# Masking x1 instead of the adjacency in the second aggregation of a two-layer graph kernel

## The chip, the cores and the metric

The kernel runs on one core of a Trainium2 chip. The core has a matrix engine (PE, with its weight loads shown apart as PEld), a vector engine (DVE), a scalar engine (ACT), a third elementwise engine (POOL) and a queue that issues transfers (SP). The time is the device time of one execution in microseconds. Before the change it is 1818.78 us, the median of three runs (1818.59 to 1822.25).

## The reference

There are 64 graphs of 256 nodes with 512 features in float32. Layer 0 aggregates x over the adjacency, divides by the degree, concatenates with x and multiplies by a weight, then adds x and normalizes. Layer 1 projects x1 to q, k and v, aggregates the masked k over the adjacency, takes the dot of q with the aggregate as a score, a softmax over the nodes of a graph, and adds the weighted v before a second normalization.

```python
def _L0_gnn_ref(x, adj, W):
    deg = jnp.sum(adj, axis=-1, keepdims=True)
    agg = jnp.einsum('bij,bjf->bif', adj, x) / jnp.maximum(deg, EPS)
    cat = jnp.concatenate([x, agg], axis=2)
    out = jnp.einsum('bnf,of->bno', cat, W)
    return jax.nn.relu(out)

def _L1_gnn_ref(X, adj, mask, Wqk, Wv):
    qk = X @ Wqk
    q, k = jnp.split(qk, 2, axis=-1)
    v = X @ Wv
    k_m = k * mask[:, :, None]
    agg = jnp.einsum('bij,bjd->bid', adj, k_m)
    w = inv_scale * mask * jnp.einsum('bid,bid->bi', q, agg)
    L = jax.nn.softmax(w, axis=1)[:, :, None] * v
    return L

x = _layernorm(x + _L0_gnn_ref(x, adj, L0_gnn_W), axis=-1)
x = _layernorm(x + _L1_gnn_ref(x, adj, nodemask, L1_gnn_Wqk, L1_gnn_Wv), axis=-1)
```

## The kernel before, in words

Graphs are handled in 32 pairs; the index j counts pairs and k the two graphs of a pair. The main loop has one pass for each pair. Pass j does layer 0 of pair j and, from the second pass on, layer 1 of pair j - 1, so two independent streams of matmuls are there to interleave. After the loop, layer 1 of the last pair is done alone.

The projections q and k of layer 1 are folded: Wqk is multiplied out once, so that layer 1 needs x1 times one 512 by 512 weight (q in the names below, `q_at`), x1 times Wv (v), and the aggregate of x1 itself over the masked adjacency (`aggs`). All products are made by a scheme of seven block products in place of eight (P1 to P7), with sums of blocks taken beforehand on DVE or POOL and sums of products taken afterwards on DVE. Most of the seven are split once more the same way (`inner`), into seven matmuls of 256 columns.

In an order string each letter is one step on PE. Lower-case i k m p q r s are the products of layer 0, a to g the seven steps of its aggregation (`gather`: u1, g2, g5, u2, u3, g3, u4). J K H Q N P L are the products of layer 1 and A to G its aggregation. A step of a product is one matmul of 256 columns (of 512 for p and H), a step of an aggregation is two of 256, one for each graph. `ORDER0` is the list of the first pass, `ORDER1` of the second, `ORDER` of all later ones, `ORDER9` of the last layer 1. `take` walks a list and calls the steps; `when` hangs work on the completion of letters (for example `start_gather0` on p, q and r, `norm0` on a to g, `dots` on B, F and K). `HOME` and `HOME9` give each product or step its bank of PE's result memory.

Nothing is issued while the lists are walked. `Plan.record` notes every operation with its engine, its cost by a small model and its dependencies. `Plan.order` then lays them out: on each engine, among the operations that can start within a short slack, the one with the earliest due time goes first. For PE the due time is the place in the recorded order, so the lists are priorities, and a step whose data is late is passed by later ones. The program order on each engine is fixed by this before the run, SP's transfers included.

In profiles, nearly all operations of DVE, ACT and POOL have line 285 (the recorder) and matmuls have line 370, so tiles tell them apart:

- `xT`, `x1T`: transposed inputs of layer 0 and layer 1; `xT_s`, `x1T_s`, `xT_i`, `x1T_i` are their block sums. `w`, `t`, `t_i` are weights and their sums.
- `adj` (two buffers, used by turns): the transposed adjacency of a pair. `sa` (two buffers): four sums of adjacency blocks. Before, buffer 0 holds the sums of the raw adjacency for layer 0, and buffer 1 those of the masked adjacency for layer 1.
- `own` (three buffers): layer 0's result, normalized to x1 in place, later the final output. `y`: layer 0's second product, later q. `tv`: the three T sums of y.
- `shared`: weights at the start and the transposed x of the second pair; later its lower half is the aggregate of layer 1 (`agg_of`), which first holds the T sums of x1, and its upper half is v (`v_of`).
- `turn`: degree rows (the adjacency loaded row-wise, summed by ACT in `degrees`), then x1 turned in 32 by 32 blocks by DVE in `norm0`, from which 16 transfers (`place`) fill `x1T`, then the row of scores that `softmax` broadcasts.

The mask is applied by `mask_adj`: ACT scales each adjacency tile in place, row by row, after layer 0's aggregation has used it; then `adj_sums(j, 1)` sums the masked blocks on POOL. For the first pair `mask_adj` is called twice; the mask here is all ones.

Of the kernel before, what the change touches and what calls it, by code (L numbers as in the profile page):

```python
# [10 lines left out]
F32 = mybir.dt.float32  # L11
BF16 = mybir.dt.bfloat16
AF = mybir.ActivationFunctionType
# [3 lines left out]
P = 128  # L17
# [12 lines left out]
HOME = "i6 k7 m7 p2 q6 r7 s6 a7 b2 c3 J3 K2 H1 Q5 N7 L7 P7 A6 B4 C5"  # L30
HOME9 = "J1 K7 H3 Q7 N6 L1 P1 A2 B3 C1"
# [289 lines left out]
def resnorm_kernel(  # L321
# [58 lines left out]
    def send(out, in_, due=None, late=0.0):  # L380
# [8 lines left out]
    (adjs, rows, xs, Xs, rdegs, sumsA, sumsM, owns, ys, aggs, vs, x1Ts, scores, columns, rows_w,  # L389
     probs) = ({} for _ in range(16))  # L390

    shared = mem.tile([P, 4 * N_SIDE], F32, name="shared")
# [4 lines left out]
    turned_rows = mem.tile([P, 2 * NT * F], F32, name="turn")  # L397
# [129 lines left out]
    def adj_sums(j, n):  # L527
        a, s = adjs[j], sa[n]
        a11, a21, a12, a22 = (a[:, :, t, h * P:(h + 1) * P] for t in range(2) for h in range(2))
        gp.tensor_add(s[:, 0], a21, a22)  # L530
        gp.tensor_sub(s[:, 1], s[:, 0], a11)
        gp.tensor_sub(s[:, 2], a11, a21)
        gp.tensor_sub(s[:, 3], a12, s[:, 1])
        return {"A11": a11, "A12": a12, "A22": a22, "S1": s[:, 0], "S2": s[:, 1], "S3": s[:, 2], "S4": s[:, 3]}

    def mask_adj(j):
        for k in range(2):
            for t in range(NT):
                act.activation(adjs[j][:, k, t], adjs[j][:, k, t], AF.Copy,
                               scale=mask_sb[:, 2 * j + k, t:t + 1])  # L540
# [88 lines left out]
    def sums_T(val, to=None):  # L629
        b11, b12, b21, b22 = (val[:, :, t, h * HF:(h + 1) * HF] for t in range(NT) for h in range(2))  # L630
        if to is None:
            tv = ring("tv", [P, 3, 2, HF])
            t2, t3, t4 = (tv[:, r] for r in range(3))
            t1 = b12
        else:
            t1, t2, t4, t3 = (to[:, :, t, h * HF:(h + 1) * HF] for t in range(NT) for h in range(2))
        if to is not None:
            vec.tensor_sub(t1, b12, b11)
        vec.tensor_sub(t2, b22, t1)
        if to is None:  # L640
            vec.tensor_sub(t3, t2, b11)
        else:
            vec.tensor_sub(t3, b22, b12)
# [144 lines left out]
    def softmax(j):  # L788
# [7 lines left out]
        row = turned_rows[:, NT * F:NT * F + P // Q * 2 * NT * (Q + 1)].rearrange("p (a c) -> p a c", a=P // Q)  # L796
# [131 lines left out]
    sumsA[0] = adj_sums(0, 0)  # L928
# [7 lines left out]
    for j in range(NP):  # L936
# [12 lines left out]
        def start_gather0():  # L949
            units.update(gather("abcdefg", sumsA.pop(j), sums_T(ys[j]), at["a"], at["c"], at["b"],  # L950
                                own=own, rdeg=rdegs.pop(j)))
# [22 lines left out]
        def next_adj():  # L974
            if j < NP - 1:
                load_adj(j + 1)
                sumsA[j + 1] = adj_sums(j + 1, 0)
# [16 lines left out]
        else:  # L994
# [37 lines left out]
            when("ikmpqrs" if j == 1 else "", lambda: T.append(sums_T(owns[j - 1], aggs[j - 1])))  # L1032
# [18 lines left out]
    T = sums_T(x1, aggs[j])  # L1051
    sumsM[j] = adj_sums(j, 1)
# [7 lines left out]
    units.update(gather("ABCDEFG", sumsM.pop(j), T, at["A"], at["C"], at["B"], aggs[j]))  # L1060
# [87 lines left out]
```

## Time and profile before

| what | value |
|---|---|
| median of three runs | 1818.78 us (1818.59 to 1822.25) |
| the profiled execution's own time | 1818.37 us |
| its span, first to last instruction | 1816.6 us |
| mean granted clock of PE | 0.999 |
| busy: PE / PEld / DVE / ACT / POOL | 1801.9 / 1439.9 / 1562.1 / 1299.2 / 1196.6 us |
| matmul records | 7724 |
| DMA share of 16 engines | 36.7% |

All durations below come from that one profiled execution. A group's line names the source line, the engine, the operation, out<-in by tile names, the shapes, the count, then busy time in us and the mean of one in ns, and after the bar the idle time just before and what ended it. Each float32 matmul leaves two records. A matmul's recorded end is modelled, so distances between starts say more than durations.

### The profile page before, as it was taken

The numbers are of one execution on the slowest core, as the hardware profiler recorded it, in microseconds if no ns is written. First come the engines' busy times: TensorE is split into PE (matmuls) and PEld (weight loads), VectorE is DVE, ScalarE is ACT, GpSimd is POOL, SyncE is SP. The second block draws the span as 40 slices with busy tenths as digits, with TensorE's granted clock in tenths as the row PEclk, the third lists the DMA queues.
The fourth block names the chain that finished last, engine by engine and source line by source line (L and its number), as shares of the span: only waits on it lengthen the run. The fifth ranks groups of instructions, "written<-read, shape, count | busy, mean of one in ns | idle before, by whom it ended". The sixth has DMA issues, their size and how long they took to land.

```text
span 1816.6 us, 27899 instructions
## 1 busy us (share of the span) xinstructions
PE 1801.9 (99%) x7724; PEld 1439.9 (79%) x7724; DVE 1562.1 (86%) x3511; ACT 1299.2 (72%) x3475; POOL 1196.6 (66%) x1729
## 2 busy tenths in 40 slices
PE   9999999999999999999999999999999999999998
PEld 5777878878888888878788788888788887788875
DVE  7888888889888889898888898898888888988886
ACT  3657876678766778766787767787667777667866
POOL 5866676766766866766767667667667666676652
PEclk9999999999999999999999999999999999999999
DMA  7134334343243443343433433433434333334312
GB/s 239 52 77 116 94 94 100 99 111 101 86 117 87 101 118 95 91 112 88 111 104 97 104 88 100 122 94 88 119 81 111 106 104 95 97 92 120 94 20 77
DMA packets 380730, 181.72 MB, mean 100 GB/s; under 512 B 263712, under 2 KB 345248, under 8 KB 380576
## 3 DMA queue, kind: packets, MB, share of 16 engines
q1 hardware_dynamic: 380576, 179.94, 36.7%
q8 instruction: 63, 1.03, 0.3%
q14 instruction: 91, 0.75, 0.1%
HBM read 114.35 MB, written 34.08 MB: 82 GB/s over the span
## 4 chain that ended last, share of the span: by engine, by line
PE 98%; DVE 1%; DMA 1%; ACT 0%; SPq 0%; issue 0%; ACTq 0%; DVEq 0%
PE bank L370 98%; DMA shared<-wqk_t 1%; DVE bank L285 0%; PE bank L376 0%; DVE own L285 0%; SPq L386 0%; ACT own L285 0%; DVE t_i L285 0%; DVE st L285 0%; DVE w L285 0%; DVE x L285 0%; DVE y L285 0%; ACT y L285 0%; ACT shared L285 0%; DVE top L285 0%
## 5 line engine op out<-in xcount | busy, mean ns | idle before, releaser
L285 DVE TENSOR_TENSOR bank<-bank,fifth 128x256 f32<-128x256 f32 x866 | 377.9, 465 | 119.0 <-ACT fifth L285 83.1
L285 ACT COPY fifth<-bank 128x256 f32<-128x256 f32 x616 | 220.0, 373 | 234.1 <-PE bank L370 232.8
L285 ACT COPY y<-bank 128x512 f32<-128x512 f32 (+1 forms) x256 | 135.5, 532 | 130.8 <-PE bank L370 112.3
L370 PE MATMUL bank<-t_i,x1T_i 128*128 128x256 f32 x748 | 207.5, 379 | 1.1 <-ACT bank L285 1.1
L285 ACT COPY shared<-bank 128x512 f32<-128x512 f32 x314 | 179.8, 594 | 36.9 <-PE bank L370 34.8
L285 ACT ACTIVATE own<-own,shift,rstd 128x512 f32<-128x512 f32 x254 | 201.0, 828 | 0.2 <-DVE shift L285 0.2
L370 PE MATMUL bank<-t_i,xT_i 128*128 128x256 f32 x760 | 195.9, 379 | 0.0
L285 DVE SCALAR_TENSOR_TENSOR own<-bank,rdeg,own 128x256 f32<-128x256 f32 x384 | 172.2, 477 | 19.3 <-PE bank L370 17.0
L285 ACT ACTIVATE junk<-own,less 128x512 bf16<-128x512 f32 x254 | 184.0, 724 | 3.1
L285 ACT COPY bank<-bank 128x256 f32<-128x256 f32 (+1 forms) x352 | 145.9, 421 | 54.9 <-PE bank L370 35.8
L370 PEld LDWEIGHTS bank<-t_i,x1T_i 128*128 128x128 f32 x748 | 140.8, 190 | 35.6 <-issue 9.0
L285 DVE TENSOR_TENSOR y<-bank,y 128x512 f32<-128x512 f32 (+1 forms) x256 | 150.6, 618 | 20.2 <-PE bank L370 17.6
L370 PE MATMUL bank<-t,x1T_s 128*128 128x512 f32 (+1 forms) x384 | 163.5, 521 | 0.6 <-DVE own L285 0.6
L285 POOL TENSOR_TENSOR shift<-less,rstd 128x2 f32<-128x2 f32 x126 | 23.1, 203 | 212.9 <-ACT rstd L285 212.6
L370 PEld LDWEIGHTS bank<-t_i,xT_i 128*128 128x128 f32 x760 | 140.4, 189 | 27.4 <-issue 1.9
L370 PE MATMUL bank<-t,xT_s 128*128 128x512 f32 (+1 forms) x384 | 159.7, 521 | 0.0
L285 DVE TENSOR_TENSOR shared<-bank,shared 128x512 f32<-128x512 f32 (+1 forms) x157 | 138.4, 883 | 9.5 <-ACT shared L285 6.8
L285 POOL TENSOR_TENSOR x1T_i<-x1T 128x256 f32<-128x256 f32 x124 | 97.2, 793 | 74.8 <-PE bank L370 71.8
L370 PE MATMUL bank<-w,x1T_i 128*128 128x256 f32 x500 | 144.5, 380 | 0.5 <-DVE bank L285 0.5
L370 PE MATMUL bank<-w,xT_i 128*128 128x256 f32 x508 | 141.2, 380 | 0.6 <-DVE bank L285 0.5
L285 POOL TENSOR_TENSOR xT_s<-xT,xT_s 128x256 f32<-128x256 f32 x62 | 65.3, 1070 | 112.2 <-PE bank L370 110.8
L285 POOL TENSOR_TENSOR sa<-adj 128x256 f32<-128x256 f32 x128 | 92.1, 729 | 59.2 <-ACT adj L285 55.0
(174 smaller groups left out, 4788.5 us busy)
## 6 DMA issues: line engine op xcount, KB each, us to landing
x<-x SPq DMA_DIRECT2D x64, 512.0 KB, 3.4
xT<-x_t SPq DMA_DIRECT2D x62, 512.0 KB, 3.3
out<-own SPq DMA_DIRECT2D x62, 512.0 KB, 3.4
x1T<-turn SPq DMA_DIRECT2D x480, 64.0 KB, 2.1
turn<-adj SPq DMA_DIRECT2D x64, 256.0 KB, 3.3
adj<-adj_t SPq DMA_DIRECT2D x64, 256.0 KB, 3.5
turn<-dram SPq DMA_DIRECT2D x31, 264.0 KB, 5.1
shared<-wqk_t SPq DMA_DIRECT2D x4, 512.0 KB, 8.4
```

Source lines behind the costliest of these rows:

```text
L285: self.plan.record(self.name, lambda: call(out, *args, **kwargs), outs, ins, busy, done, port)
L370: plan.record("PE", lambda: nc.tensor.matmul(ps, a, b, start=start, stop=True, skip_group_check=True), [ps], [a, b], busy, busy + 0.165, w ...
```

## The change

Layer 1's aggregation takes the raw adjacency and its raw sums, which layer 0 has already used, and multiplies them with masked x1. A new tile `masked` holds three masked blocks of x1 (B11, B21, B22), written by ACT with the mask as a per-row scale: per graph one activation of 256 columns and one of 512. T1 is masked x12 minus B11 by one DVE operation per graph; T2, T3 and T4 are plain subtractions as before, written where the aggregate will stand. `mask_adj` and the second call of `adj_sums` go, and the two `sa` buffers are used by turns. The `tv` buffer goes; the T sums of y are put in the first columns of `turn`, and the softmax row moves behind them. Degree rows are loaded to `shared` instead of `turn` from the fourth pair on. All four order strings and some bank places are new; every list has the same letters the same number of times.

```diff
-HOME = "i6 k7 m7 p2 q6 r7 s6 a7 b2 c3 J3 K2 H1 Q5 N7 L7 P7 A6 B4 C5"
-HOME9 = "J1 K7 H3 Q7 N6 L1 P1 A2 B3 C1"
+HOME = "i6 k7 m7 p0 q6 r7 s6 a7 b2 c3 J3 K2 H2 Q5 N7 L7 P7 A6 B4 C5"
+HOME9 = "J6 K7 H4 Q0 N6 L0 P7 A2 B3 C1"
...
-ORDER0 = ("k i k i k i i k i k i i k p k p m m m m q q s m m p p r r m r q r r r s r q a b s s d e c f g")
-ORDER1 = ("i k i i k i i i i k k k p m m k k m m p m p q m m r p r r q r q q q q r q s r s s r s s a J J J "
-          "J J s b s d e c J J f H K K H Q H K H K K K Q Q g N N K A N D P Q C E G N N N N P P L L L B L P "
-          "L F L L")
-ORDER = ("i k i i i k k i k i k i k m k p p p m m q m m r p r r m m r r r q q r q q q J q s J J s s s J J "
-         "s a b d s s J e c J H f K K H K H g K K H K K Q Q A N Q N Q Q D N N C Q Q N P N E P N P P G P P "
-         "P L F L B L L L L L")
-ORDER9 = ("J J J J A J J C J D K B K K H K E H F G N H N H K Q Q K N P N N Q N Q N P K P P L S L Z L L")
+ORDER0 = ("i i k i k k i k i k k i k i p p m q p q p m m m m r r s r q s m r r q r r s a m b d s e c f g")
+ORDER1 = ("i i k i k i i k k k i k i p k m p m m p m m r m m p q r r r q r q r q q q q r J J a s J b s s J "
+          "s J s s d s e c f J g J K K K K K H N K K H N A N D N N N H Q Q H Q C E Q N G L P F B L L L L P "
+          "P L L P")
+ORDER = ("i k k i i i i k k k i k i m m p k p m m p m m p m q r q r q r r r r q r J q q q s s s s s a b d "
+         "s J s e J J J g c J J f K H K K K K H K N K H N H Q Q Q Q N N A N Q Q Q D N C N E G P P F B P P "
+         "P P L L L L L L L P")
+ORDER9 = ("J J J A J J D C B J E G J N H K H H K H K Q F Q N N Q K K N K N Q K P N P N L P P L S Z L L")
...
+    masked = mem.tile([P, 2, 3, HF], F32, name="masked")
...
-    turned_rows = mem.tile([P, 2 * NT * F], F32, name="turn")
+    N_T, N_ROW = 3 * 2 * HF, P // Q * 2 * NT * (Q + 1)
+    turned_rows = mem.tile([P, N_T + N_ROW], F32, name="turn")
...
-        rows[j] = turned_rows[:, :2 * NT * N].rearrange("p (k t n) -> p k t n", k=2, t=NT)
+        rows[j] = (shared if j > 2 else turned_rows)[:, :2 * NT * N].rearrange("p (k t n) -> p k t n", k=2, t=NT)
...
-    def adj_sums(j, n):
-        a, s = adjs[j], sa[n]
+    def adj_sums(j):
+        a, s = adjs[j], sa[j % 2]
...
-    def mask_adj(j):
-        for k in range(2):
-            for t in range(NT):
-                act.activation(adjs[j][:, k, t], adjs[j][:, k, t], AF.Copy,
-                               scale=mask_sb[:, 2 * j + k, t:t + 1])
...
+    def masked_T(j):
+
+        t1, t2, t4, t3 = (aggs[j][:, :, t, h * HF:(h + 1) * HF] for t in range(NT) for h in range(2))
+        b11, b21, b22 = (masked[:, :, r] for r in range(3))
+        x1 = owns[j]
+        for k in range(2):
+            m = mask_sb[:, 2 * j + k]
+            act.activation(b11[:, k], x1[:, k, 0, :HF], AF.Copy, scale=m[:, 0:1])
+            act.activation(masked[:, k, 1:].rearrange("p r f -> p (r f)"), x1[:, k, 1], AF.Copy, scale=m[:, 1:2])
+            vec.scalar_tensor_tensor(t1[:, k], x1[:, k, 0, HF:], m[:, 0:1], b11[:, k],
+                                     op0=OP.mult, op1=OP.subtract)
         vec.tensor_sub(t2, b22, t1)
+        vec.tensor_sub(t3, t2, b11)
         vec.tensor_sub(t4, b21, t2)
         return {"B11": b11, "B21": b21, "B22": b22, "T1": t1, "T2": t2, "T3": t3, "T4": t4}
+
+    def sums_T(val):
+        b11, b12, b21, b22 = (val[:, :, t, h * HF:(h + 1) * HF] for t in range(NT) for h in range(2))
+        tv = turned_rows[:, :3 * 2 * HF].rearrange("p (r k f) -> p r k f", r=3, k=2)
+        t2, t3, t4 = (tv[:, r] for r in range(3))
+        vec.tensor_sub(t2, b22, b12)
+        vec.tensor_sub(t3, t2, b11)
+        vec.tensor_sub(t4, b21, t2)
+        return {"B11": b11, "B21": b21, "B22": b22, "T1": b12, "T2": t2, "T3": t3, "T4": t4}
...
-        sq = turned_rows.rearrange("p (b k c t q) -> p b k c t q", b=P // Q, k=2, c=NF, t=NT)
+        sq = turned_rows[:, :2 * NT * F].rearrange("p (b k c t q) -> p b k c t q", b=P // Q, k=2, c=NF, t=NT)
...
-        row = turned_rows[:, NT * F:NT * F + P // Q * 2 * NT * (Q + 1)].rearrange("p (a c) -> p a c", a=P // Q)
+        row = turned_rows[:, N_T:].rearrange("p (a c) -> p a c", a=P // Q)
...
-            mask_adj(j)
...
-                sumsA[j + 1] = adj_sums(j + 1, 0)
+                sumsA[j + 1] = adj_sums(j + 1)
...
-                    mask_adj(0)
...
-                sumsM[j - 1] = adj_sums(j - 1, 1)
...
-                units.update(gather("ABCDEFG", sumsM.pop(j - 1), T[0], at["A"], at["C"], at["B"],
+                units.update(gather("ABCDEFG", sumsA.pop(j - 1), T[0], at["A"], at["C"], at["B"],
...
-            when("ikmpqrs" if j == 1 else "", lambda: T.append(sums_T(owns[j - 1], aggs[j - 1])))
+            when("ikmpqrs" if j == 1 else "", lambda: T.append(masked_T(j - 1)))
...
-    T = sums_T(x1, aggs[j])
-    sumsM[j] = adj_sums(j, 1)
+    T = masked_T(j)
...
-    units.update(gather("ABCDEFG", sumsM.pop(j), T, at["A"], at["C"], at["B"], aggs[j]))
+    units.update(gather("ABCDEFG", sumsA.pop(j), T, at["A"], at["C"], at["B"], aggs[j]))
```

More of the change, by code (lines that the diff above doesn't have):

```diff
@@ L387, in send @@
         step.due = step.due if due is None else due
-    (adjs, rows, xs, Xs, rdegs, sumsA, sumsM, owns, ys, aggs, vs, x1Ts, scores, columns, rows_w,
-     probs) = ({} for _ in range(16))
+    (adjs, rows, xs, Xs, rdegs, sumsA, owns, ys, aggs, vs, x1Ts, scores, columns, rows_w,
+     probs) = ({} for _ in range(15))
+    masked = mem.tile([P, 2, 3, HF], F32, name="masked")
     shared = mem.tile([P, 4 * N_SIDE], F32, name="shared")
@@ L627, in outer @@
         return [unit(e) for e in range(H)]
[L629 to L638, printed above, removed]
+    def masked_T(j):
[8 more added lines that the diff above has]
+                                     op0=OP.mult, op1=OP.subtract)
         vec.tensor_sub(t2, b22, t1)
[L640 to L643, printed above, removed]
+        vec.tensor_sub(t3, t2, b11)
         vec.tensor_sub(t4, b21, t2)
         return {"B11": b11, "B21": b21, "B22": b22, "T1": t1, "T2": t2, "T3": t3, "T4": t4}
+    def sums_T(val):
[6 more added lines that the diff above has]
+        return {"B11": b11, "B21": b21, "B22": b22, "T1": b12, "T2": t2, "T3": t3, "T4": t4}
     def gather(names, a, w, u, p5, c, dst=None, own=None, rdeg=None):
@@ L927, in resnorm_kernel @@
     inner_sums(Xs[0], "P2")
-    sumsA[0] = adj_sums(0, 0)
+    sumsA[0] = adj_sums(0)
     degrees(0)
@@ L949, in start_gather0 @@
         def start_gather0():
-            units.update(gather("abcdefg", sumsA.pop(j), sums_T(ys[j]), at["a"], at["c"], at["b"],
+            units.update(gather("abcdefg", sumsA[j], sums_T(ys[j]), at["a"], at["c"], at["b"],
                                 own=own, rdeg=rdegs.pop(j)))
```

## The prediction

> **What bounds the kernel now.** I read the page's first part, then busy time by stretches, then the matmuls one by one in order of time, then who waited for whom, then the groups by shape, and the transfers in order of time.
>
> ```profile
> PE 1801.9 (99%) x7724; PEld 1439.9 (79%) x7724; DVE 1562.1 (86%) x3511; ACT 1299.2 (72%) x3475; POOL 1196.6 (66%) x1729
> ```
>
> PE is the engine to watch; but a busy share can hide slow running. The stretches, each line start:end, length, then busy time of each engine, say where PE has gaps:
>
> ```profile
> 0.00:13.70 13.70, 12.07 (x26) 4.80 (x26) 5.62 (x14) 1.28 (x1) 1.39 (x8) 1.00 0.90 301
> 13.70:72.00 58.30, 57.72 (x224) 39.97 (x224) 49.55 (x94) 34.42 (x94) 46.31 (x63) 1.00 0.46 156
> 72.00:127.30 55.30, 51.86 (x204) 37.07 (x203) 47.37 (x96) 27.75 (x63) 35.45 (x48) 1.00 0.27 62
> 127.30:1721.10 1593.80, 1593.71 (x6914) 1293.83 (x6913) 1385.42 (x3136) 1171.85 (x3152) 1075.02 (x1555) 1.00 0.38 101
> 1776.40:1807.50 31.10, 30.20 (x116) 19.93 (x114) 21.80 (x51) 22.30 (x56) 7.69 (x13) 1.00 0.23 72
> 1807.50:1816.60 9.10, 1.08 (x3) 0.25 (x2) 4.49 (x14) 3.64 (x12) 0.00 (x0) 0.78 0.31 115
> ```
>
> From 127.3 to 1721.1 us, nearly 29 of the 32 pairs, PE lacks 0.09 us of 1593.80, at a granted clock of 1.00. What it lacks elsewhere, between first weights and last matmuls: 58.30 - 57.72 = 0.58, 55.30 - 51.86 = 3.44 in the second pair's stage, 31.10 - 30.20 = 0.90 in the last pair's second layer. Is a full PE also a fast one? In order of time:
>
> ```profile
> 851.74 0.59 PE L370 MATMUL bank<-y,adj 128*128 128x256 f32 x2
> 852.17 0.59 PE L370 MATMUL bank<-t_i,xT 128*128 128x256 f32 x2
> 852.60 0.59 PE L370 MATMUL bank<-y,adj 128*128 128x256 f32 x2
> ```
>
> Starts of two-record matmuls are 0.43 us apart, without a slip. A pair's list has 106 letters: 84 of one 256-column matmul (0.432), 14 gather units of two (0.863), 8 of one 512-column matmul (0.86): 36.3 + 12.1 + 6.9 = 55.2 us. The same place of successive pairs comes 55.32 us apart. So the steady pair already lasts as long as its matmuls, and the change leaves every matmul in place: 106 letters of the same kinds in each list, before and after.
>
> The Trainium skill (Perfetto Trace Analysis, Identifying the Most-Contended Engine) calls matmul busy time no good measure of headroom and points to the weight loads' busy share instead. Here that is 79%, so by that rule an estimated fifth of the span, some 380 us, would be open to a better order; the 0.43 us rhythm of the starts decides against it.
>
> Where the 3.44 us lie:
>
> ```profile
> 89.65 0.70 PE L370 MATMUL bank<-tv,adj 128*128 128x256 f32 x2 [1.25 <-DVE own L285]
> 90.93 0.70 PE L370 MATMUL bank<-t,x1T_s 128*128 128x256 f32 x2 [0.58 <-DVE own L285]
> ...
> 93.01 1.13 PE L370 MATMUL bank<-w,x1T_i 128*128 128x256 f32 x4 [0.53 <-DVE bank L285]
> 95.23 0.67 PE L370 MATMUL bank<-t_i,x1T_i 128*128 128x256 f32 x2 [1.09 <-ACT bank L285]
> ```
>
> These four holes are 3.45 us, all at the end of the second pair's first aggregation. DVE and ACT idle there as well (ACT 27.75 of 55.30): it is an order that ran dry, not an engine that is full.
>
> **The change part by part.**
>
> ```profile
> L285 POOL TENSOR_TENSOR sa<-adj 128x256 f32<-128x256 f32 x128 | 92.1, 729 | 59.2 <-ACT adj L285 55.0 <-PE bank L370 4.2
> L285 ACT ACTIVATE adj<-adj,mask_sb 128x256 f32<-128x256 f32 x132 | 67.5, 517 | 3.6 <-PE bank L370 3.2
> L285 DVE TENSOR_TENSOR shared<-own,shared 128x512 f32<-128x512 f32 x64 | 47.1, 736 | 0.1
> L285 DVE TENSOR_TENSOR shared<-own 128x512 f32<-128x512 f32 x64 | 44.9, 701 | 1.8
> ```
>
> *Second sums of the masked adjacency go (POOL).* Three POOL groups write sa: 92.1, 50.0 and 47.2 us; half is the second set, 94.7 us, 2.96 a pair of POOL's 37.4. No matmul of the steady stretch waits for them: zero on the path. DVE's 512-column adds took from 0.68 to 1.38 us in one pair; if POOL's adds beside them are what stretches some, DVE gains between 0 and 2.96 us a pair, none of it on PE's path.
>
> *ACT masks x1 in place of adj.* 132 x 0.517 = 67.5 us go (4 a pair and 4 more for the first pair). Four a pair come: two of 256 columns (0.517) and two of 512. No 512-column activation with one column scale stands in the trace; a copy of 512 takes 0.585 and a scale-and-shift 0.828, these are the ends. I take 0.73, the 256 row plus the copies' step (0.585 - 0.373). 2 x 0.517 + 2 x 0.73 = 2.5 a pair, 80 us in all: ACT +12 us (0.4 a pair), of 40.5 busy in 55.3. Hidden by ACT's idle 14.8; if that were gone it would cost its 0.4 a pair, 13 us.
>
> *T sums of x1 (DVE).* Before 2 x 0.736 + 2 x 0.701 = 2.87 a pair. After three of 512 (2.1 to 2.2) and two scalar_tensor_tensor of 256; nearest row, the same operation of 256 from a bank, 0.477. Together 3.1, +0.2 a pair, ends -0.1 (at the 0.43 of a 256-column add) and +0.6 (at 0.68, the fastest 512-column one). DVE is busy 48.3 of 55.3: hidden.
>
> The Trainium skill (Vector Engine (DVE) Microarchitecture Reference, Points that are easy to get wrong) says that a scalar_tensor_tensor with two SBUF sources that are not bf16 runs at half rate, which speaks against this part. By it the two would take an estimated 0.75 us each and DVE 0.5 more a pair. The 512-column one with two such sources (own from shared, probs, own) took 0.743 us, where plain adds of that size took 0.70: this trace shows no halving.
>
> *A new wait for these sums.* From the fourth pair on, degree rows land in the half of shared where T1 to T4 of k = 0 are then written. The queue of one steady pair (its stage starts at 831.7):
>
> ```profile
> 831.46 11.77 SPq L386 DMA_DIRECT2D x1T<-turn  x16
> 843.33 0.56 SPq L386 DMA_DIRECT2D dram<-turned  x1
> 843.99 0.91 SPq L386 DMA_DIRECT2D turn<-adj  x2
> ```
>
> Rows issue 12.3 us into the stage and land 3.3 later; ACT read them for their sums at 20.5 to 26. The rows' transfer must now follow the last dots with shared (832.4 to 837.3): 844.0 - 837.3 = 6.7 us of cover; behind it on SP wait softmax's row and the next xT, which it doesn't delay. But the T sums, before at 833.8 to 840.1 (2 to 8 us in), can only run after ACT has read the rows, and gather1 first needs them at 875.9 (44 us in). They move into these stretches:
>
> ```profile
> 831.70:841.70 10.00, 10.00 (x46) 8.21 (x45) 8.72 (x23) 5.48 (x12) 4.79 (x8) 1.00 0.69 154
> 841.70:857.70 16.00, 16.00 (x69) 12.58 (x69) 13.15 (x28) 8.07 (x29) 14.85 (x21) 1.00 0.35 69
> 857.70:875.70 18.00, 18.00 (x78) 14.30 (x77) 16.25 (x41) 16.40 (x47) 8.45 (x12) 1.00 0.44 147
> ```
>
> If rows are read as late as now, 3.1 us of DVE work meet 18.00 - 16.25 = 1.75 free: 1.35 us too much. If ACT reads them as they land (it idles half of the stretch before), 2.85 more are free and all fits. So the cost is 0 to 1.35 us a pair, below zero excluded since PE is full. I take 0: cover 4.6 against 3.1, and the aggregation's last letter comes at 30 us where it came at 34, which brings its DVE work forward (places by the lists).
>
> *T sums of y into turn.* Same three instructions. They must follow the last x1T transfer out of turn (843.2 + 2.1 = 845.3); the first tv sum ran at 853.0: 7.7 us of cover. The list now ends with P, and x1T transfers overwrite what P's last matmul reads. Before, that letter stood at 50.0 and its matmul (t_i, x1T) ran at 885.4, 53.7 in; now it stands at 54.8, so between 0.3 us into the next stage, and 4 with the same lag, where the transfers started at -0.24 (DVE's turning held them, up to 831.3). That takes 0.5 to 4 of the 7.7, and of the 8 us between landing and the first J (853.5). Behind them on SP wait softmax's row and the degree rows, which slide along. Cost 0. In the first two pairs degree rows share turn with these sums; rows of the second pair were issued by 44 us and are read before the first pair's sums are due: 0 to +1, taken 0. Softmax's row has its own columns, as before apart from them.
>
> *adj loads.* They wait for the last of G and B: nominally 50 us in, before 53. Earlier, no cost.
>
> *New orders.* In the steady pairs PE cannot gain (0.09 us is all) and can only lose. The second pair's hole of 3.44 lies just where the list is rewritten (s ends before c; J and K are spread behind g): from all of it gone to as much again. I take half, -1.7, between a hole that no full engine asks for and a chain (matmul, DVE, next matmul on the same bank) that holds 1.25 us of it and stays. Last pair: A now stands behind three J instead of four and needs masked x1; the last scaling by ACT before it ended at 1775.0, A ran at 1776.5, the added ACT pieces are 0.52 and 0.73 on an ACT that is full there: -0.9 to +1.3, taken 0, as its 0.90 lie elsewhere (softmax at 1802).
>
> Sum against the profiled execution's own 1818.37 us (span 1816.6, 1.8 around it): -1.7 gives 1816.7. The median of the three runs, 1818.78, is 0.4 above it: 1817.1, I say 1817.
>
> **The rivals.**
> *All small holes close.* 0.58 + 3.44 + 0.90 = 4.92 go: 1818.78 - 4.92 = 1813.9. For it: none is forced by a full engine. Against: the first 0.58 waits for weight sums that do not change, and the 0.90 for softmax's latency. It is also the floor, unless the last 9.1 us shrink.
> *Slower: the T sums of x1 behind the degree rows crowd DVE* between 26 and 44 us of each steady pair, and bank additions that PE waits for come late. Price up to 1.35 us in each of 29 pairs, 39 us; at 0.3 us, 8.7: 1827.5. It decides from 3.64 / 29 = 0.13 us a pair. For it: DVE and ACT are 90% full there, and a list with no slack turns any delay into idle PE. Against: ACT can read the rows 4 us earlier, and POOL has 2.96 us a pair less to do beside DVE.
> *The ends get worse:* the hole grows or the tail waits for masked x1, +1 to +5: about 1821.
> *The change does nothing:* POOL, ACT and DVE parts all hidden and the hole as before: 1818.8, inside the first case.
>
> **How the numbers follow.** Likeliest, steady stretch full and part of the hole gone: 0.44, at 1817, own range 1814.3 to 1819.7. All holes closed: 0.19. DVE crowded: 0.28. Ends worse: 0.09. A measurement tells about 0.2%, 3.64 us, from no change: faster means under 1815.1, slower over 1822.4. Faster: 0.19 + 0.08 of the likeliest = 0.27. Slower: 0.27 of the crowded case and 0.06 of the worse ends = 0.33. Same: the rest, 0.40. The range 1812.8 to 1830 takes in the floor with a microsecond of tail, and the crowded case up to 0.39 us a pair; some 0.05 is left below and 0.12 above.
>
> **What will show it.** Right: groups sa of 64 + 32 + 32 instead of 128 + 64 + 64 instructions; no activation of adj by mask_sb; masked written by 128 activations of 0.5 to 0.75 us; PE idle under 1 us between 127 and 1721; the holes near 90 us smaller. Wrong: a wait of PE for DVE or ACT that recurs every 55 us, pairs more than 55.4 us apart, T sums of shared from own running just before gather1, or holes at 88 to 98 us larger than 3.4.

## The result and the profile after

The changed kernel takes 1823.18 us (median, 1822.56 to 1823.62) where the kernel before takes 1818.67; the ratio is 1.0021, with a 95% interval of 1.0015 to 1.0028. The profiled execution has a span of 1821.2 us against 1816.6. So the change costs some 4.5 us, inside the range of the forecast, but with the other sign than its 1817. Three of the 15 executions of the kernel before took 1822.3 to 1822.5 us and the others at most 1819.0; the trace of run i further down is of such a long one (granted clock 0.91 between 72 and 127 us), and only its later, steady pairs at clock 1.00 are read.

The page's busy line:

```profile
PE 1805.4 (99%) x7724; PEld 1432.9 (79%) x7724; DVE 1561.5 (86%) x3543; ACT 1331.0 (73%) x3471; POOL 1084.0 (60%) x1601
```

The busy times moved in the directions foretold, though not by the sizes: POOL has 113 us less, ACT 32 more, DVE the same. The groups of the new operations, over the whole execution:

```profile
L285 POOL TENSOR_TENSOR sa<-adj 128x256 f32<-128x256 f32 x64 | 46.9, 735 | 91.4 <-PE bank L370 51.2 <-DMA adj<-adj_t 40.2
L285 ACT ACTIVATE masked<-own,mask_sb 128x512 f32<-128x512 f32 x64 | 45.7, 722 | 10.8 <-PE bank L370 9.2
L285 ACT ACTIVATE masked<-own,mask_sb 128x256 f32<-128x256 f32 x64 | 29.4, 511 | 1.5 <-DVE shared L285 1.5
L285 DVE SCALAR_TENSOR_TENSOR shared<-own,mask_sb,masked 128x256 f32<-128x256 f32 x64 | 32.1, 502 | 0.0
L285 DVE TENSOR_TENSOR shared<-masked,shared 128x512 f32<-128x512 f32 x64 | 59.0, 922 | 0.1
L285 DVE TENSOR_TENSOR shared<-shared,masked 128x512 f32<-128x512 f32 x32 | 25.5, 798 | 0.0
```

The sums of adjacency blocks are halved in number, the masked copies take 0.722 and 0.511 us (0.73 and 0.517 had been taken), T1 by a scalar_tensor_tensor 0.502 (0.477). Only the 512-column T sums are longer than foretold, 0.92 and 0.80 against some 0.7; why is seen below.

The same stretches as before (start:end, length, then busy time of PE, PEld, DVE, ACT, POOL with counts, the clock, the DMA share and GB/s):

```profile
13.70:72.00 58.30, 57.22 (x220) 39.41 (x221) 51.20 (x97) 32.52 (x90) 43.68 (x58) 1.00 0.46 155
72.00:127.30 55.30, 55.30 (x226) 41.10 (x225) 44.98 (x97) 30.16 (x70) 36.10 (x52) 1.00 0.26 63
127.30:1721.10 1593.80, 1590.37 (x6875) 1279.69 (x6874) 1382.44 (x3153) 1198.38 (x3137) 967.17 (x1432) 1.00 0.37 100
1500.00:1650.00 150.00, 148.14 (x635) 117.60 (x634) 129.82 (x298) 106.95 (x284) 86.33 (x130) 1.00 0.36 94
```

The hole of the second pair is gone altogether: 55.30 of 55.30, where 3.44 us were missing. But the long stretch, which lacked 0.09 us, now lacks 3.43. Four single holes make up 3.1 of that; they don't recur from pair to pair (the bracket is PE's idle time just before and what it waited for):

```profile
187.73 0.48 PE L370 MATMUL bank<-t,xT 128*128 128x256 f32 x1 [0.53 <-DVE bank L285]
217.69 0.45 PE L370 MATMUL bank<-t_i,x1T_i 128*128 128x256 f32 x1 [0.72 <-DVE bank L285]
1598.97 0.45 PE L370 MATMUL bank<-shared,sa 128*128 128x256 f32 x1 [0.66 <-ACT fifth L285]
1635.19 0.48 PE L370 MATMUL bank<-w,x1T_i 128*128 128x256 f32 x1 [1.20 <-DVE bank L285]
```

A second loss is not in these busy times at all. In the 1100 us between 400 and 1500 PE is shown as busy without a gap in both kernels, yet it finishes 4765 matmul records after and 4776 before: at 0.216 us each, 2.4 us less work. The kernel before, then the changed one:

```profile
400.00:1500.00 1100.00, 1100.00 (x4776) 894.08 (x4775) 961.25 (x2169) 806.64 (x2173) 743.34 (x1075) 1.00 0.38 101
400.00:1500.00 1100.00, 1100.00 (x4765) 886.23 (x4764) 952.54 (x2183) 830.18 (x2171) 672.14 (x993) 1.00 0.38 101
```

Successive pairs stand 55.45 us apart, 0.13 more than the 55.32 before. Going through the starts of the matmuls, four of a pair come 0.05 to 0.07 us late, always the same four; before there was one. Each stands behind a weight load that was held up:

```profile
512.68 0.19 PEld L370 LDWEIGHTS bank<-w,xT_s 128*128 128x128 f32 x1 [0.20 <-issue]
516.63 0.19 PEld L370 LDWEIGHTS bank<-w,xT_i 128*128 128x128 f32 x1 [0.20 <-issue]
540.83 0.19 PEld L370 LDWEIGHTS bank<-t_i,x1T_i 128*128 128x128 f32 x1 [0.18 <-POOL x1T_i L285]
557.72 0.19 PEld L370 LDWEIGHTS bank<-t_i,xT_i 128*128 128x128 f32 x1 [0.19 <-ACT bank L285]
```

0.068 + 0.061 + 0.047 + 0.054 = 0.23 us a pair, less the 0.067 of the one that was there before (w, xT_s, too): 0.16 by this count, 0.13 by the pairs' distance, since two delays of some 0.02 that the kernel before had are gone. Together: hole closed -3.4, single holes +3.1, 27 pairs by 0.13 +3.5, first stretch +0.5. That makes 3.7 of the 4.6 us between the spans. Setting the n-th matmul record of one trace against the n-th of the other shows where the changed kernel stands in between: 3.8 us ahead at 130 us, where the hole has closed, 0.7 ahead at 411, 2.3 behind at 1575 (3.0 lost in 21 pairs), and 4.6 behind at 1689, past the last two holes.

The question is therefore what makes the four late loads and the single holes: the new orders, the new data flow, or an engine beside PE.

### The profile page after: what moved, and what is told of

Same layout as the page of the kernel before. It is cut to its first block, busy times and chain, and to the rows that moved or that the text cites. A ratio compares the mean times of both kernels' runs of the same rounds, so it can differ in the third digit from the quotient of the medians.

```text
span 1821.2 us, 27394 instructions
## 1 busy us (share of the span) xinstructions
PE 1805.4 (99%) x7724; PEld 1432.9 (79%) x7724; DVE 1561.5 (86%) x3543; ACT 1331.0 (73%) x3471; POOL 1084.0 (60%) x1601
## 4 chain that ended last, share of the span: by engine, by line
PE 96%; DVE 2%; ACT 1%; DMA 1%; issue 0%; SPq 0%; DVEq 0%; ACTq 0%
PE bank L370 95%; DMA shared<-wqk_t 1%; DVE bank L285 0%; DVE y L285 0%; ACT junk L285 0%; DVE turn L285 0%; ACT fifth L285 0%; ACT own L285 0%; PE bank L376 0%; SPq L386 0%; DVE own L285 0%; ACT y L285 0%; ACT bank L285 0%; DVE t_i L285 0%; ACT shared L285 0%
## 5 line engine op out<-in xcount | busy, mean ns | idle before, releaser
L285 DVE TENSOR_TENSOR bank<-bank,fifth 128x256 f32<-128x256 f32 x866 | 382.8, 465 | 103.9 <-ACT fifth L285 60.7
L285 POOL TENSOR_TENSOR x1T_i<-x1T 128x256 f32<-128x256 f32 x124 | 90.1, 737 | 280.9 <-PE bank L370 274.1
L370 PE MATMUL bank<-t_i,x1T_i 128*128 128x256 f32 x748 | 201.1, 381 | 0.8 <-DVE bank L285 0.7
L285 ACT ACTIVATE own<-own,shift,rstd 128x512 f32<-128x512 f32 x254 | 196.1, 810 | 2.3 <-POOL shift L285 2.1
L370 PE MATMUL bank<-t,xT_s 128*128 128x512 f32 (+1 forms) x384 | 167.6, 521 | 0.4 <-ACT bank L285 0.4
L370 PEld LDWEIGHTS bank<-t_i,x1T_i 128*128 128x128 f32 x748 | 136.9, 189 | 31.0 <-POOL x1T_i L285 4.0
L285 ACT COPY own<-bank 128x512 f32<-128x512 f32 x192 | 112.7, 588 | 52.8 <-PE bank L370 49.3
L370 PE MATMUL bank<-w,x1T_i 128*128 128x256 f32 x500 | 148.4, 380 | 1.2 <-DVE bank L285 1.2
L285 POOL TENSOR_TENSOR xT_s<-xT,xT_s 128x256 f32<-128x256 f32 x62 | 45.5, 734 | 170.1 <-PE bank L370 156.7
L370 PE MATMUL bank<-w,x1T 128*128 128x256 f32 (+1 forms) x392 | 118.9, 388 | 0.0
```

Source lines behind the costliest of these rows:

```text
L285: self.plan.record(self.name, lambda: call(out, *args, **kwargs), outs, ins, busy, done, port)
L370: plan.record("PE", lambda: nc.tensor.matmul(ps, a, b, start=start, stop=True, skip_group_check=True), [ps], [a, b], busy, busy + 0.165, w ...
```

## The experiments

**Order and data flow apart (a to d).** Theory L puts the loss on the strings, theory F on the data flow. Runs a and d give the kernel before new strings; b and c give the changed kernel old ones.

```diff
a, on the kernel before:    HOME, HOME9, ORDER0, ORDER1, ORDER, ORDER9 of the changed kernel
b, on the changed kernel:   the same six strings of the kernel before
c, on the changed kernel:   as b, but ORDER0 and ORDER1 stay new
d, on the kernel before:    ORDER0 and ORDER1 new, the rest old
```

> The data flow of before with the six order and place strings of after. If the loss lies in the new lists (theory L: the steady list leaves more weight loads a tenth of a microsecond short, four in a pair instead of one), pairs come 55.4 to 55.5 us apart and the time is 1821 to 1825 us, with the 3.44 us hole near 90 us gone. If it lies in the new data flow (theory F: T sums of x1 that wait for the degree rows, sums crowded on DVE beside POOL), pairs come 55.32 apart and the time is 1813 to 1816.

> The data flow of after with the strings of before. Theory L: 1817 to 1820 us, pairs 55.3 us apart, the hole near 90 us of some 3.4 back. Theory F: pairs 55.4 or more apart and single holes beside long DVE adds, 1822 to 1828, since the loss stays and the gain of the hole is gone.

> The data flow of after with ORDER0 and ORDER1 of after, all other strings of before. Theory L: the hole is gone and the steady pairs are as before, 1813 to 1816 us. Theory F: 1820 to 1824, as after, since the steady pairs keep the new data flow.

> The data flow of before with ORDER0 and ORDER1 of after, all else of before. Both theories: 1813 to 1816 us, the 3.44 us hole gone, steady pairs 55.32 apart. If the hole stays (1818.7), its end needs the raw adjacency sums as well as the list.

Measured: a 1847.49 us, ratio 1.015 (1.0135 to 1.0165). b 1889.64, 1.0379 (1.0365 to 1.0394). c 1889.49, 1.0379 (1.0365 to 1.0393). d 1818.55, 0.9992 (0.9983 to 1.0001).

Both theories fall. New strings alone cost 29 us, the new data flow alone 71, both together 4.5: each order fits its own data flow. In b nearly every pair has two waits of PE behind late sums of x1. The timeline of b around one of them:

```profile
855.52 1.54 DVE L281 TENSOR_TENSOR shared<-masked,shared 128x512 f32<-128x512 f32 x1
857.11 1.13 PE L366 MATMUL bank<-shared,sa 128*128 128x256 f32 x4 [0.48 <-DVE shared L281]
860.04 0.67 DVE L281 TENSOR_TENSOR shared<-shared,masked 128x512 f32<-128x512 f32 x1
860.63 0.67 DVE L281 TENSOR_TENSOR shared<-masked,shared 128x512 f32<-128x512 f32 x1
861.79 1.10 PE L366 MATMUL bank<-w,x1T_i 128*128 128x256 f32 x4 [1.39 <-DVE bank L281]
```

The T sums run directly in front of the aggregation that needs them, and the bank additions queued behind them on DVE come late: the mechanism of the forecast's slower rival, in an order that isn't the changed kernel's. Run d has half of the second pair's hole left (0.52 and 1.09 us at 92 to 95 us) and a new wait of 1.32 at 65 us. a has the same three, b a wait of 1.7 us and c, with the new ORDER0 and ORDER1, one of 1.9 at 93 us. Of these kernels only the one with all six new strings and the new data flow closes the hole.

**What delays the sums under the old strings (e, f).** In e the masking is left out; in f the degree rows have a buffer of their own besides.

```diff
e, on b:
-    masked = mem.tile([P, 2, 3, HF], F32, name="masked")
...
-        b11, b21, b22 = (masked[:, :, r] for r in range(3))
...
+        b11, b12, b21, b22 = (owns[j][:, :, t, h * HF:(h + 1) * HF] for t in range(NT) for h in range(2))
+        vec.tensor_sub(t1, b12, b11)
f, on e:
+    own_rows = mem.tile([P, N_SIDE], F32, name="rows")
...
-        rows[j] = (shared if j > 2 else turned_rows)[:, :2 * NT * N].rearrange("p (k t n) -> p k t n", k=2, t=NT)
+        rows[j] = (own_rows if j > 2 else turned_rows)[:, :2 * NT * N].rearrange("p (k t n) -> p k t n", k=2, t=NT)
```

> The changed kernel with the strings of before, and with the masking of x1 left out: the T sums of x1 are taken from x1 itself (T1 by one subtraction of 512 columns), the tile of masked blocks is gone; the mask's values are all one. Degree rows still land where the T sums of x1 are written. Theory 'rows' (the T sums are late because they stand behind the degree rows in the same buffer): the two holes of 1.55 and 0.65 us in each pair stay, 1880 to 1892 us, pairs 57.6 to 58.0 us apart. Theory 'masking' (they are late because of the scaled copies and the two-operand step ahead of them): the holes go, 1818 to 1830 us.

> As the run beside it (strings of before, masking left out), and the degree rows have a buffer of their own from the fourth pair on, so that the T sums of x1 wait for nothing but x1 and the last reader of the aggregate. Theory 'rows': the T sums run within 10 us of the normalization again, no wait in front of the second aggregation, pairs 55.3 to 55.5 us apart, 1816 to 1826 us, some 65 us less than the run beside it. Theory 'masking': no difference to the run beside it (within 3 us).

e took 1865.77 us, ratio 1.0255 (1.0239 to 1.027); f 1868.50, 1.027 (1.0256 to 1.0284). The masked copies and T1's longer operation are worth 24 of b's 71 us. Taking the degree rows out of the way gains nothing: under the old strings theory "rows" falls, though the forecast had built its rival on it. What the other 47 us are was not taken apart further.

**What delays loads in the changed kernel: work taken away under an unchanged order (g, h, j; i on the kernel before).** From the fifth to the 29th pair a kind of instruction is planned as ever, so that all engines keep their order, but not issued.

```diff
         for s in self.order():
-            self.tc.keep_in_program_order(s.issue())
+            if not s.dropped:
+                self.tc.keep_in_program_order(s.issue())
...
+        step.dropped = 4 <= self.at <= 28 and ...
g, i: engine == "POOL" and to.startswith(("xT", "x1T", "sa"))
h:    engine == "ACT" and to.startswith("masked")
j:    both
```

> The changed kernel, its instructions in the same order on every engine, but from the fifth to the 29th of the 32 pairs POOL's block sums are not issued (the products read the sums left from earlier pairs, so the output isn't the reference's). Theory 'contention' (DVE's adds stretch beside POOL's, so a bank or a sum comes about 0.1 us late, four times in each pair, and now and then 0.5 us): the short waits go, pairs 55.45 to 55.32 us apart, the single hole near 1599 us goes, 1819 to 1820.5 us, ratio to before 1.000 to 1.001. Theory 'list' (the four places are tight by the order alone, whatever POOL does): pairs 55.43 to 55.45 us apart, 1822.5 to 1823.5 us, ratio 1.002.

> The changed kernel, its instructions in the same order on every engine, but from the fifth to the 29th pair ACT's scaled copies of x1 into the masked blocks are not issued (the T sums read the blocks left from an earlier pair, so the output isn't the reference's): 2.5 us of ACT less in each pair. Theory 'ACT is crowded' (two of the four short waits end with an ACT copy that stands behind the new copies): those two waits go, 0.10 us a pair, 1820.3 to 1821 us, ratio 1.001. Theory 'contention' or 'list': the copies run at a time when nothing is short of ACT, nothing changes, 1822.5 to 1823.5 us, ratio 1.002 to 1.003.

> The kernel before, its instructions in the same order on every engine, but from the fifth to the 29th pair POOL's block sums are not issued (stale sums are read, so the output isn't the reference's). In the changed kernel the same cut took 6 us. Theory 'the new order is exposed to POOL' (POOL stretches DVE's adds in both kernels, but only the new order has waits of PE behind such adds): before gains little, 1817.5 to 1818.9 us, ratio 0.999 to 1.000, pairs 55.31 to 55.32 us apart. Theory 'POOL costs any order the same': 1812 to 1814 us, ratio 0.997.

> The changed kernel with the same order on every engine, and from the fifth to the 29th pair neither POOL's block sums nor ACT's scaled copies into the masked blocks are issued (stale blocks are read, so the output isn't the reference's). Theory 'two causes' (three of the four short waits of a pair hang on DVE or ACT work late by POOL, the fourth on an ACT copy late by the new scaled copies): the two gains add, 6.1 + 1.8 less what they share, 1815 to 1816 us, ratio 0.998, pairs 55.31 to 55.34 us apart. Theory 'one cause' (the copies matter only through POOL): 1816.8 to 1817.4 us, as without POOL's sums alone.

| run | us | ratio to before (95%) | late matmuls a pair | pairs apart |
|---|---|---|---|---|
| changed kernel | 1823.18 | 1.0021 (1.0015 to 1.0028) | 4 | 55.45 |
| g, no POOL sums | 1817.12 | 0.9987 (0.9978 to 0.9996) | 2 | 55.33 |
| h, no masked copies | 1821.34 | 1.0012 (1.0003 to 1.0021) | 3 | 55.39 |
| j, neither | 1815.57 | 0.9977 (0.9968 to 0.9986) | 1 | 55.27 |
| i, before without POOL sums | 1816.77 | 0.9989 (0.9980 to 0.9998) | 0 | 55.25 |

h takes away one late load, the one at 557.72, which waits for a copy by ACT: ACT's new work costs 1.8 us, where 2.2 to 2.9 had been expected with two loads hanging on it. g takes away the three others and the single holes behind 300 us, and 6.1 us, where theory "contention" had 2.7 to 4.2; one late load of 0.053 us comes in elsewhere. In j the gains add. i gains 2.2 us, more than theory "exposed" allowed and less than the same 6: the one late load of the kernel before is gone, and pairs are 0.064 us closer, 1.6 us in 25 pairs. So POOL's sums cost either order something, the new one 3.9 us more. With ACT's 1.8, the two holes ahead of the cut pairs (1.25) and the first stretch (0.5), less the closed hole (3.4), that is 4.1 of the 4.5 us between the kernels.

**Another order of the letters (k, l).** Only ORDER differs; the letters of k:

```diff
-ORDER = ("i k k i i i i k k k i k i m m p k p m m p m m p m q r q r q r r r r q r J q q q s s s s s a b d "
...
+ORDER = "k i k i i k k k i i i i p k m k m p p m m m m p q m r r q r r r r q q q r q q s s a s s J s b s s J J J J d e c J g J f K K K H K K K N H K N H Q H Q N N Q A Q Q Q Q D P N C E N N P G P F P P L P L B L L P L L L"
```

> The changed kernel complete, with another order of the letters in ORDER alone (same letters, same counts), chosen so that fewer PE steps have their last input ready just as PE comes to them. Theory 'the loss is near misses of the list, not the new work': a list with fewer of them gets the steady pairs to 55.32 to 55.40 us apart and the time to 1816 to 1821 us, ratio 0.998 to 1.001. Theory 'the new data flow costs it in any order': 1822 to 1828 us.

> As the run beside it with a second order of the letters in ORDER. Theory 'near misses of the list': 1816 to 1823 us, ratio 0.998 to 1.002. Theory 'the new data flow costs it in any order': 1822 to 1828 us.

k took 1831.47 us, ratio 1.0063 (1.005 to 1.0075), l 1840.25, 1.0111 (1.0097 to 1.0124). With these two orders the output isn't the reference's, so they are no kernels to keep; the number of instructions on each engine is unchanged. They settle neither theory. They show that with the same work the list alone moves the time by 8 and 17 us against the changed kernel.

**What in POOL's sums it is (m).** g had taken away three things at once: POOL's load beside DVE, the lateness of its sums, and one of two waits in front of the loads. The trace's own rows for one place (start, duration, engine, instruction, names, semaphores waited for or raised; 100 is raised by DVE, 99 by POOL) show the third:

```
changed kernel
512.492 0.691 DVE   TENSOR_TENSOR    y<-bank,y
512.508 0.379 PE    MATMUL           bank<-w,xT
512.610 0.051 PEld  EVENT_SEMAPHORE  $S[100]>=
512.685 0.187 PEld  LDWEIGHTS        bank<-w,xT_s   $S[99]>=
512.724 0.448 PE    MATMUL           bank<-w,xT_s
g
843.354 0.691 DVE   TENSOR_TENSOR    y<-bank,y
843.369 0.379 PE    MATMUL           bank<-w,xT
843.485 0.186 PEld  LDWEIGHTS        bank<-w,xT_s   $S[100]>=
843.585 0.385 PE    MATMUL           bank<-w,xT_s
```

The load must wait for DVE and for POOL. It carries one wait itself; the other is an instruction of its own ahead of it, 0.051 us long. DVE's release is that of the addition before y, 0.09 us after y's start in both; POOL's last release ahead of the load is at 512.415, before DVE's at 512.581, so POOL's sum is not late here. From y's start to the load it is 0.193 us with two waits and 0.131 with one. The loads at 516.63 and 540.83 have such an instruction ahead of them too, as has the late load of the kernel before. The Trainium skill (Perfetto Trace Analysis, Identifying Dependency Chains) says that for an instruction waiting on several engines such instructions may be put in front; the rows agree, with one of 0.051 us.

m leaves the waits and takes away the load: each of POOL's sums handles one column of each block.

```diff
+            to = outs[0].tensor.name
+            if self.name == "POOL" and 4 <= self.plan.at <= 28 and to.startswith(("xT", "x1T", "sa")):
+                first = lambda ap: ap[(slice(None),) * (len(ap.shape) - 1) + (slice(0, 1),)]
+                small = [first(a) for a in (outs[0], *ins)]
+                self.plan.record(self.name, lambda: call(*small, **kwargs), outs, ins, busy, done, port)
+                return
```

> The changed kernel, the same order on every engine, but from the fifth to the 29th pair each of POOL's block sums handles only the first column of each block, so that PE's weight loads still wait for POOL's semaphore while POOL is nearly idle (the other columns are stale, so the output isn't the reference's). Without these sums it took 1817.1 us, with them 1823.2. Theory 'second wait' (a weight load that waits for two engines is preceded by an instruction that only waits, and starts some 0.06 us later; without POOL's sums three of the four late loads of a pair have only one wait): the short waits are back, 1819.5 to 1821.5 us, pairs 55.40 to 55.45 us apart. Theory 'POOL is busy' (its sums come late, or stretch DVE's adds): 1816.8 to 1817.6 us, as without the sums.

m took 1820.09 us, ratio 1.0001 (0.9993 to 1.001). All four late loads are back at the same places and of the same size (0.068, 0.060, 0.047, 0.056), pairs are 55.45 us apart, and the single holes in the cut pairs stay away. Stretches of m:

```profile
127.30:1721.10 1593.80, 1592.28 (x6888) 1282.76 (x6888) 1351.46 (x3158) 1201.20 (x3142) 344.92 (x1432) 1.00 0.38 100
1500.00:1650.00 150.00, 150.00 (x646) 120.04 (x646) 126.04 (x302) 109.36 (x292) 38.30 (x133) 1.00 0.38 98
```

Between 1500 and 1650 nothing is missing, where the changed kernel lacked 1.86 us; most of the 1.52 us that the long stretch still lacks are the two holes before the cut begins. So the 6.1 us of g fall into two halves. 1820.09 - 1817.12 = 3.0 us are the second wait of three loads in 25 pairs, net of the one late load that comes in with g. 1823.18 - 1820.09 = 3.1 us are POOL being busy, and matched by number, the matmuls of the two traces part almost only in three places: 0.5 us between 357 and 373 us, 0.8 at 1598.97 and 1.4 at 1635.19. In the pairs between 411 and 1575 busy POOL costs PE nothing. What busy POOL does is seen in DVE's groups between 400 and 1500 us. Changed kernel:

```profile
L285 DVE TENSOR_TENSOR bank<-bank,fifth 128x512 f32<-128x512 f32 x80 | 55.8, 697 | 10.9 <-ACT fifth L285 10.7
L285 DVE TENSOR_TENSOR shared<-masked,shared 128x512 f32<-128x512 f32 x40 | 37.7, 943 | 0.0
L285 DVE TENSOR_TENSOR turn<-y 128x512 f32<-128x512 f32 x20 | 20.4, 1019 | 0.0
```

m:

```profile
L292 DVE TENSOR_TENSOR bank<-bank,fifth 128x512 f32<-128x512 f32 x80 | 55.8, 697 | 12.9 <-ACT fifth L292 10.7
...
L292 DVE TENSOR_TENSOR shared<-masked,shared 128x512 f32<-128x512 f32 x40 | 27.3, 683 | 0.0
L292 DVE TENSOR_TENSOR turn<-y 128x512 f32<-128x512 f32 x20 | 13.8, 692 | 0.0
```

In these two groups, adds with both sources in SBUF, the core's working memory, one takes 0.68 to 0.69 us with little work on POOL and on average 0.94 to 1.02 with all of it; an add with a source in a bank takes 0.70 in either case. The largest single hole is this at its worst, in the changed kernel's timeline:

```profile
1630.50 1.28 POOL L285 TENSOR_TENSOR x1T<-x1T 128x512 f32<-128x512 f32 x1
1631.73 1.27 POOL L285 TENSOR_TENSOR x1T_s<-x1T_s,x1T 128x512 f32<-128x512 f32 x1
1631.80 3.00 DVE L285 TENSOR_TENSOR turn<-y 128x512 f32<-128x512 f32 x1
1632.96 0.88 POOL L285 TENSOR_TENSOR x1T_i<-x1T_s 128x128 f32<-128x128 f32 x2
1634.71 0.75 DVE L285 TENSOR_TENSOR bank<-bank,fifth 128x256 f32<-128x256 f32 x2
```

The T sum of y starts just behind a POOL sum and takes 3.00 us, during which POOL goes through its series (the last sum starts at 1634.32); the bank addition queued behind it is 2.3 us late, and PE waits 1.20 at 1635.19. The Trainium skill (SBUF — State Buffer, Who interferes with whom) has the rule: a DVE instruction with two SBUF inputs contends with a POOL instruction that reads SBUF, and one with at most one SBUF input, outside the 2-port modes, doesn't. All these groups agree with it.

**Can the late loads be ordered away (n, o, p).** Steps are moved in the finished order of the changed kernel, in every steady pair alike, where no data forbids it. n has one move: behind the load of 512.68 stands the step of the same product that reads xT_i, ready 2 us earlier; it goes ahead. o and p have twelve each.

```diff
+MOVES = (('PE', 113, 1),)
...
     def issue(self):
-        for s in self.order():
+        for s in self.moved(self.order()):
```

> The changed kernel complete, with one edit of PE's order: in each steady pair the product step that reads xT_i and stands directly behind one of the four late loads (w, xT_s) goes ahead of it. Its own data are there 2 us before. Theory 'late loads': that wait of 0.068 us goes in some 25 pairs, 1821.0 to 1822.0 us, pairs 0.06 to 0.07 us closer. Theory 'the waits only move': 1822.5 to 1823.5 us.

> The changed kernel complete, with twelve moves of single steps by one to three places in the steady pairs, on PE (six), DVE (three), POOL (two) and ACT (one), each chosen so that a load of PE has its data earlier; nothing else is changed and no dependency is broken. Theory 'late loads of the order': at least two of the four short waits of a pair go, pairs 55.31 to 55.38 us apart, 1816.5 to 1821 us, ratio 0.999 to 1.001. Theory 'the new data flow costs it in any order': 1822 to 1828 us.

> As the run beside it with a second set of twelve moves (PE seven, ACT three, DVE two). Theory 'late loads of the order': 1817 to 1821.5 us, ratio 0.999 to 1.0015. Theory 'the new data flow costs it in any order': 1822 to 1828 us.

n took 1830.67 us, ratio 1.0061 (1.0049 to 1.0073); o 1853.18, 1.0183 (1.017 to 1.0196); p 1846.98, 1.0148 (1.0135 to 1.0161). All three lost, n by 7.5 us against the changed kernel. In n the late load is gone, and 0.9 us further on there is a new one. Weight loads of n:

```profile
849.75 0.37 PEld L395 LDWEIGHTS bank<-t_i,xT_i 128*128 128x128 f32 x2
850.62 0.73 PEld L395 LDWEIGHTS bank<-t_i,xT_i 128*128 128x128 f32 x4 [0.49 <-DVE bank L310]
```

The step moved back by 0.43 us (w, xT_s) is read by an addition of DVE, which now starts at 850.13, and the load at 850.62 waits for that: 0.257 and 0.104 us lost where 0.068 was saved, 0.29 a pair. "The waits only move" was nearer than "late loads", and the waits also grew. Among the kernels that compute the whole reference none is faster than the one before by more than its interval; d is level with it.

## Why the prediction was right or wrong

*Steady stretch at cost 0 (wrong; the failing step).* "In the steady pairs PE cannot gain ... and can only lose", and then nothing was charged. It lost 3.5 us in the 27 or so steady pairs and 3.1 in single holes: three loads with a second wait (m against g, 3.0 us), an ACT copy made late by the masked copies (h, 1.8), and POOL being busy (the changed kernel against m, 3.1), at the two largest places by a DVE sum that runs into POOL's; 1.6 us have to be set against these for the one load with a second wait that the kernel before has. The premise was off already: the starts before are not "without a slip", that one load a pair was 0.067 us late. Hiding was judged by free time of engines in stretches of 10 to 18 us, and none of the added pieces filled its engine; but a load on time starts only 0.10 us ahead of its matmul (843.485 and 843.585), and what counts is whether that is overrun. The forecast put the deciding point at 0.13 us a pair, and the pairs are 0.13 longer; that is a coincidence, since the mechanism is another than its rival named.

*Second pair's hole, taken half gone, -1.7 (right in kind, mis-sized).* It closed whole: -3.4. Runs a to d show that it needs the new order and the new data flow together.

*T sums of x1 behind the degree rows, taken 0, rival up to 1.35 us a pair (the size held, the reason did not).* They do run late, spread over 40 us (726.7 to 767.8 in one pair) where all ran within 6, and yet in the steady pairs of the changed kernel none of the four late loads waits for them. Under the old strings (b) they do hold PE, but f shows that the degree rows are not the reason.

*POOL -94.7 us, said to give DVE 0 to 2.96 us a pair (right, but not its weight for PE).* POOL lost 113 us, 95 of them in the sums of adjacency blocks. How far its sums stretch DVE's work is seen by taking them away, first from the kernel before (i), then from the changed one (g):

```profile
400.00:1500.00 1100.00, 1100.00 (x4778) 897.58 (x4777) 918.36 (x2167) 806.61 (x2174) 13.82 (x80) 1.00 0.39 101
400.00:1500.00 1100.00, 1100.00 (x4777) 890.27 (x4776) 931.02 (x2193) 832.12 (x2175) 23.24 (x80) 1.00 0.38 101
```

DVE has 961.25 - 918.36 = 42.9 us more with the sums before, and 952.54 - 931.02 = 21.5 after: half as much, some 1.1 us a pair less. Yet PE got nothing from it, because other pieces now meet POOL: before, the stretched adds held up no matmul (matched by number, i parts from the kernel before in the steady pairs almost only at the one late load), while after, a T sum of x1 stretched to 1.80 us stands ahead of the hole at 1598.97 and one of y, 3.00 us, ahead of that at 1635.19. In m neither is stretched, and both holes are gone. Less contention in sum was taken as less harm.

*T sums of x1 on DVE, +0.2 us a pair, ends -0.1 and +0.6 (too small).* The low end should have been about +0.1 (2.1 + 2 x 0.43 = 2.96 against 2.87). Measured are 59.0 + 25.5 + 32.1 = 116.6 us, 3.64 a pair, +0.8: T1 was right to about 5%, the three 512-column sums were stretched. That used up what DVE gained elsewhere, so its busy time stayed, 1562.1 and 1561.5.

*ACT +12 us, hidden (nearly).* The busy time grew by 32, but the new copies take 45.7 + 29.4 = 75.1 us where the scaling of adj took 67.5 (a busy time; 132 x 0.517 is 68.2), and the durations of all ACT instructions add up to only 7.7 more. The rest of the 32 is less overlap between neighbouring records, not work. h prices the copies at 1.8 us, mainly the one load that waits for an ACT copy.

*T sums of y in turn, softmax's row, adj loads, tail: 0.* No wait of PE in the steady pairs names one of these transfers; the tail moved by less than 1 us. *The half rate that the Trainium skill (Vector Engine (DVE) Microarchitecture Reference, Points that are easy to get wrong) has for such a scalar_tensor_tensor, by the forecast's estimate 0.75 us:* 59 of the 64 took under 0.49 us, again no halving.

*What will show it.* Groups sa of 64 + 32 + 32, masked by 128 activations of 0.5 to 0.75 us and the smaller hole came. "PE idle under 1 us between 127 and 1721" did not, and the sign it gave for a wrong forecast, pairs more than 55.4 us apart, did: 55.45.

## What to carry to other kernels

When PE is full, added work on other engines is not free because they have idle time; ask which of PE's loads have their last input within 0.1 us of the moment they are needed, and what the change does to those. A busy share of 100% hides such losses: count matmuls finished in a fixed time, or measure the distance of the same step in successive loops. A finely ordered schedule is fitted to its data flow; either half alone cost 29 and 71 us here, and a single swap 7.5.

## What the runs showed of the hardware

A weight load that must wait for two engines got a separate 0.051 us instruction in front and started about 0.06 us later than with one wait; three such loads in 25 pairs cost 3.0 us net (m against g). A 512-column float32 add of DVE with both sources in SBUF took 0.68 us with little work on POOL (m) and up to 3.00 beside a row of POOL sums (changed kernel), while adds from a bank kept 0.70 on average.
